# A transformer block on one core: turning the LayerNorm tiles of the feed-forward parts with VectorE blocks and DMAs through DRAM instead of TensorE

## The chip, the core and the metric

The kernel runs on one core of a Trainium2 chip. The core has five engines that run side by side, each with its own instruction stream in program order: TensorE (PE, matrix products; its weight loads are shown as PEld), VectorE (DVE), ScalarE (ACT), GpSimd (POOL) and SyncE (SP, which here issues DMAs). They meet by semaphores. Sixteen DMA engines move data between DRAM, the on-chip memory SBUF and, for the engines alone, the accumulator memory PSUM, which has 8 banks of 128 x 512 fp32. The metric is the device time of one execution in microseconds; the time given is a median of runs.

## The reference

All is fp32. Input x is (8, 256, 512): 8 sequences of 256 tokens, 512 features. Four residual parts follow each other:

```
x = x + attn_a(layernorm(x))    # 32 heads of 16, 8 key/value heads, rotary, causal softmax
x = x + ffn(layernorm(x))       # base linear 512x512 + bias, top-2 of 8 experts, LoRA of rank 16
x = x + attn_b(layernorm(x))    # same shape, other weights
x = x + ffn(layernorm(x))       # the same ffn weights again
```

`layernorm` has no learned factors: (x - mean) / sqrt(var + 1e-5) over the features. `ffn` forms gate logits (8 per token), takes the two largest, softmaxes them, and adds 2 * sum over experts of weight * (x A_e) B_e to x base + b. The factor 2 needs no instruction of its own: the two weights are formed against half of their sum.

## The kernel before, in words

**Units and tiles.** Work is cut into 16 units, each one attention part and the feed-forward part behind it, for one sequence: units 0 to 3 are the first attention of sequences 0 to 3, 4 to 7 the second attention of the same, 8 to 15 the same for sequences 4 to 7. Each unit has two tiles of 128 tokens (t = 0, 1). So there are 64 LayerNorm tiles: 32 ahead of attentions ("a") and 32 ahead of feed-forwards ("f").

**A LayerNorm tile** (`layernorm_t`, L623). VectorE takes mean and variance (L631, L633, L635), GpSimd raises to the power -1/2 (L637), VectorE forms the shift (L638), ScalarE writes the normalized 128 x 512 tile xn (L640). A product needs the features on the partitions, so the tile has to be turned: PE makes four 128 x 128 transposes into a PSUM bank (L647), and ScalarE copies the bank into xnT (for "a") or yT (for "f") (L654). There are 3 xn buffers and 2 yT buffers.

**Attention** (`attention`, L658). PE forms keys (L675), values (L686) and queries (L746); VectorE and GpSimd rotate them (L700 to L768); DMAs copy q and parts of the values (L720, L775). Scores are formed twice: once to find the row maxima (PE L801, ScalarE copy L816, GpSimd mask L832, VectorE maximum L846, turned by PE L855, copied by ScalarE L858 and put into q by two DMAs, L862), and once with the maxima in place (PE L887, ScalarE exponential L902, GpSimd mask L913). PE multiplies by the values (L932); ScalarE copies the result to e (L947). The sums of the softmax go by DMA to a small tile (sums, L952), through a reciprocal (L955), by DMA to DRAM (recd, L959) and by DMA back, broadcast (rec, L963); VectorE scales e (L966, L970). PE makes the `wo` product (L978) and VectorE adds it to x (L985).

**Feed-forward** (`ffn`, L989). After the LayerNorm tile comes the bias (GpSimd L994), the gate and low-rank product `gl` (PE L999, copy L1007), a short chain of gating on VectorE and ScalarE (L1018 to L1044), a transpose `lwT` (PE L1049, copy L1053), the base product (PE L1063), the low-rank product `lora` into the same bank (PE L1069), and the sum into x (DVE L1079). yT is read by `gl` and by base.

**What sets the order.** Nothing is issued directly: `plan.add` records 2,955 operations, each with its engine, a cost, what it reads and writes, and the buffers that it takes from and gives back to pools (x, xn, yT, e, big, the PSUM banks, alone or in pairs, and more). `Plan.schedule` then goes through time with these costs, and on each engine picks the ready operation with the smallest rank of a table (`RANKS`); it also deals out buffers as they come free. The instructions are issued in the order so found, so each engine's order is fixed ahead of the run. On SP the DMAs stand in the same way in one line, up to eight outstanding, and a DMA that waits for its data holds those behind it.

Of the kernel before, what the change touches and what calls it, by code (L numbers as in the profile page):

```python
# [15 lines left out]
P = 128  # L16
# [10 lines left out]
CHANGE = {"full": 0.08, "score": 0.16, "value": 0.13}  # L27
APART = 0.07
WINDOW = 3.4
SPLIT = 16  # L30
FIXED = 1.65
QUEUED = 8
# [3 lines left out]
RANKS = """  # L36
0 65 400 0 585 195 130 455 260 680 716 752 788 390 1870 955 2165 3555 325 3195 1105 1655 2615 2760
715 3645 1030 1795 2830 520 650 1240 1520 2905 1725 2255 2685 1280 1338 1680 1738 0 100 200 300 400
500 615 637 676 761 335 396 406 430 491 521 609 680 413 474 484 508 567 597 736 810 1676 1945 1852
2084 2150 2187 2277 2410 2345 2346 2373 2444 2566 2525 2657 2607 876 1407 1609 1674 1796 2515 1053  # L40
1230 1432 1497 1514 2150 3485 3130 2800 2922 3015 3259 3392 3532 3313 3435 3528 3779 3942 4228 4060
3741 3956 3863 4105 4216 4388 4514 4124 4411 4246 4565 4644 4743 4414 4779 4536 4977 5056 5142 5024
5235 5331 5266 5434 5644 5740 5675 5913 6035 6128 6237 6349 6203 6325 6418 6588 6797 6371 6511 6604
6527 6805 6712 6728 6991 6898 7100 7212 7105 7262 7371 7436 7710 7789 7854 8059 7571 8439 8920 9311
6914 7339 7550 7659 7724 8405 8450 8515 8735 8025 9203 9383 9931 9372 9654 9664 9893 9992 10057
10329 10400 11025 10882 11003 11037 11089 11072 11161 11301 11212 11456 11585 11672 11771 10472
12243 12372 10005 10066 10076 10428 10598 10683 10836 10907 11281 11560 11789 11823 11952 11858
11988 12039 12059 12079 12088 12347 12454 11075 12632 12824 1133 1194 1204 1228 1287 1317 1584 1655
824 885 895 919 978 1008 1630 1705 2038 2307 2214 2425 2723 2760 2642 3325 3260 2669 2811 2882 3271
3180 3312 3221 2897 3090 3353 3292 3525 3652 2446 2623 2872 2937 3005 3132 3870 3940 4927 5049 5142  # L50
5262 5522 5713 5229 5351 5444 5655 5766 6163 5995 5623 5745 5838 6004 6115 6522 6354 7487 7643 7736
7845 7924 8090 7237 7457 7364 7566 7645 7804 6620 6697 6728 6793 8328 8574 8605 8670 7781 7996 7903
8105 8371 10039 10254 10161 10480 10689 10978 11202 11109 11463 11585 11678 10375 10590 10497 11152
11436 11694 11859 11968 12033 12233 12405 12340 12610 12168 12990 13178 13600 11834 12009 12166
12470 12275 12670 12780 12715 13010 12698 13390 13590 13965 13829 13890 13900 14611 14932 14967
15090 15208 15067 15814 15935 15969 16021 16004 16057 16108 16128 16148 16157 16720 16763 15426
17193 17306 14026 14087 14097 14480 14539 14845 14947 15039 14933 16624 16745 16836 16947 16871
16983 17054 17034 17074 17083 17374 17411 16829 17479 17620 1055 1116 1126 1150 1211 1241 2400 2475
2794 2855 2865 2953 3059 3108 3267 3362 3472 4031 3648 4149 4302 4339 4327 4215 4280 4354 4423 4494
4872 4913 4679 4629 4573 4750 5025 4964 5135 5395 3838 4221 4449 4682 4723 4850 5594 5529 8080 8202  # L60
8295 9084 9217 9433 8177 8481 8388 8664 8846 9142 8974 8533 8655 8748 9782 10051 10832 10304 8823
9078 8985 9545 9624 9710 9286 9408 9501 9703 9945 10083 11451 11491 11702 11572 11439 11476 11507
11637 12141 12268 12361 12470 12582 12535 12750 12657 12859 13479 14993 15115 15258 14480 14752
14609 15329 15451 15544 15653 15765 14037 14248 14422 14357 14839 14884 14949 15154 14867 15534
17664 18055 16007 16198 16355 16529 16464 16737 16782 16847 17052 16765 17445 19336 19790 18116
18177 18187 18238 18362 18530 18943 19014 18655 19702 19823 19912 20106 20264 20213 20435 20308
20590 20599 22493 22549 20029 22630 23042 19851 20168 20178 20234 20295 20325 20681 20765 20415
20837 21048 21228 21309 21263 21493 21661 21681 21729 22387 22602 22720 21779 22754 22903 1898 1959
1969 1993 2052 2134 3410 3621 2998 3072 3082 4053 4289 4339 4511 4729 7589 7878 7987 8105 8311 8348
8344 8171 8236 10024 8525 8775 8853 8894 8935 9171 5052 5446 5648 5934 5877 8217 8356 8630 8848 8913  # L70
8957 9418 9617 9552 9749 9871 9964 10162 10295 10611 12829 13044 12951 13188 13368 13539 13661 13081
13330 13237 13883 14148 14434 14266 14185 14434 14341 14663 14742 14945 13940 14155 14062 14330
14532 14618 15790 15827 15858 15923 15802 15842 15988 16053 16330 16550 16457 16659 16771 18122
18244 18337 18446 18782 19895 20126 20219 16732 16854 16967 19798 20013 19920 20122 20286 19086
19297 19406 19471 20185 20230 20295 20500 19699 20880 22143 22660 20490 20949 21114 21223 21288
21701 21746 21811 22016 21544 22782 22944 23440 22721 23025 23035 23072 23164 23194 23334 23405
23304 23477 23832 23896 23948 23944 24068 24119 24371 24391 24400 24650 24693 23589 24759 24918
23501 23588 23598 23668 23931 23968 24138 24256 24056 24554 24675 24709 24761 24744 24797 24868
24848 24888 24897 25211 25248 24863 25320 25449 12433 12494 12504 12694 12811 12843 13035 13137
12885 12946 12956 13068 13195 13423 13544 13615 16432 17281 17386 17504 17570 17759 18211 17570  # L80
17635 18361 18140 18290 18602 18643 18480 18430 14577 14770 15166 15231 15248 17697 14287 15152
15354 15419 15436 17570 17831 17896 19234 19390 19483 19592 19725 19947 20393 20515 20608 20717
20828 20999 21060 22505 22627 22738 22847 22961 23103 23177 20740 20955 20862 21064 21143 21272
21089 21329 21216 21438 21517 22166 23322 23362 23573 23443 23937 24040 24071 24136 24041 24163
24306 24415 24541 24662 24877 24784 24986 25195 25564 25798 25705 25223 25345 25438 25859 25981
26074 26183 26295 25424 25612 25786 25721 25986 26031 26096 26301 26014 26681 26863 27238 26246
26437 26594 26768 26703 27172 27282 27217 27487 26968 27867 28705 29096 27299 27360 27370 27394
27453 27483 27838 28085 27571 29631 29842 29910 29962 29945 29998 30049 30346 30366 30375 30598
30635 29743 30877 30999 29157 29218 29228 29254 29482 29512 30091 30162 29617 30719 30930 30964
31016 31060 31069 31120 31140 31160 31169 31253 31303 30234 31520 31675 31077 31753 17367 17428  # L90
17438 17462 17607 17637 18030 18101 17681 17742 17752 17824 17925 17955 18076 18151 21191 21480
21589 21707 21797 21834 22262 21941 21876 21788 22191 22289 22408 22367 22499 22449 18412 18766
19029 18968 19118 21911 18219 18589 18791 18856 18991 22471 22634 22699 22847 23062 22969 23171
23535 23675 23380 23667 23502 23776 23887 24007 24203 32094 32216 32309 32531 32960 33246 33078
35089 35309 35216 35418 35497 35641 34669 34893 34800 35002 35120 35206 33420 33710 33806 33741
36489 36607 36638 36703 36913 37035 37128 37237 37349 37256 37471 37378 37642 38125 37909 38062
38155 38947 39162 39069 38512 38634 38727 38836 38948 38609 38820 38994 38929 39234 39381 39316
39631 39262 40135 40422 40914 39522 39713 39870 39979 40044 40379 40481 40546 40751 40195 41274
41422 41813 40975 41036 41046 41098 41460 41584 41788 41859 41754 42295 42416 42450 42512 42485
42548 42740 42599 42760 42769 42994 43037 41931 43205 43318 41874 41935 41945 42105 42164 42194  # L100
42391 42462 42367 42898 43019 43053 43105 43088 43141 43212 43192 43232 43241 43293 43330 42534
43402 43531 43410 43609 23362 23423 23433 23483 23562 23595 23949 24055 22964 23345 23355 23431
23575 23760 23995 24105 26671 27398 27305 27555 27621 27658 28318 27686 27621 28655 27867 28345
28423 28464 28555 28505 25666 25956 26235 26174 26407 28006 24200 24377 24579 24644 24661 27698
28205 28140 28608 28730 28823 28932 29121 29261 29071 29286 29193 29395 29506 29849 29681 29534
29656 29749 29858 29969 30285 30117 30965 31087 31180 31289 31368 31454 30137 30352 30259 30461
# [112 lines left out]
class Plan:  # L219

# [30 lines left out]
    def prepare(self):  # L259
# [3 lines left out]
        for n, o in enumerate(ops):  # L263
            for d in o[4]:
                self.succ[d].append(n)
# [886 lines left out]
```

## Time and profile before

| | |
|---|---|
| median of 3 runs | 775.36 us (774.79 to 775.76) |
| profiled execution | 773.26 us, span 771.6 us |
| PE busy | 756.0 us, 98% |
| VectorE, ScalarE, GpSimd busy | 505.9, 486.7, 513.6 us (66, 63, 67%) |
| transposes of the 64 LayerNorm tiles (L647) | 256 matmuls, 38.7 us of summed durations |
| copies out of PSUM to yT (L654) | 32, 18.9 us |
| DMA traffic | 36.06 MB, mean 47 GB/s |

The page gives busy time by engine, a chain of work followed back from the last instruction, and groups of instructions with their idle time before and what ended it. Matmuls are pipelined, so summed durations of a group are more than the time that it holds PE. "SPq" rows are DMAs as SP issues them: their duration is that of the issue, not of the transfer. Idle time of an engine other than the one that bounds the kernel costs nothing in itself.

### The profile page before, as it was taken

Reading aid. Unit: us, or ns where it says so; the run is one execution under the profiler, and the core shown is the slowest. Engines: PE = TensorE matmul, PEld = TensorE weight load, DVE = VectorE, ACT = ScalarE, POOL = GpSimd, SP = SyncE. Lnnn points to the kernel's source line nnn. Section 1 sums busy time; section 2 is a strip of 40 time slices with the busy share of each in tenths; the row PEclk is TensorE's granted clock in tenths of the full one; section 3 lists DMA queues with packets and bytes.
Section 4 is the critical chain, followed back from the end, with each engine's and each line's share of the span. In section 5 each row is a group of like instructions: output and inputs, shape, how many; then the busy total and the mean of one; then the engine's idle time right before and its main releaser. Section 6 shows DMA issues by size and latency. Waiting matters only on the chain.

```text
span 771.6 us, 17960 instructions
## 1 busy us (share of the span) xinstructions
PE 756.0 (98%) x7196; PEld 410.9 (53%) x7196; DVE 505.9 (66%) x1035; ACT 486.7 (63%) x700; POOL 513.6 (67%) x495
## 2 busy tenths in 40 slices
PE   8999999999999999999999999999999989999998
PEld 7874555556456464555555465455555434544354
DVE  6574895856698358666557469465975894666564
ACT  4687757756666654685657566764576775657631
POOL 5898894848667586586738467696468974764530
PEclk9999999999999999999999999999999999999999
DMA  9820101101010020202021210020011100110111
GB/s 298 226 77 6 35 28 38 45 16 33 17 48 5 18 61 2 76 31 62 2 72 48 71 49 3 4 62 16 16 34 51 42 4 18 49 44 32 45 32 54
DMA packets 46755, 36.06 MB, mean 47 GB/s; under 512 B 28496, under 2 KB 31568, under 8 KB 46672
## 3 DMA queue, kind: packets, MB, share of 16 engines
q1 hardware_dynamic: 46128, 34.89, 15.0%
q8 instruction: 56, 0.92, 0.5%
q14 instruction: 27, 0.22, 0.1%
q10 hardware_dynamic: 544, 0.03, 0.0%
HBM read 19.71 MB, written 4.72 MB: 32 GB/s over the span
## 4 chain that ended last, share of the span: by engine, by line
PE 89%; DVE 4%; ACT 3%; issue 2%; POOL 2%; DMA 1%; SPq 0%; POOLq 0%; ACTq 0%; DVEq 0%
PE banks L746 14%; PE banks L1063 13%; PE banks L978 13%; PE banks L887 10%; PE banks L932 9%; PE banks L801 9%; PE banks L675 4%; PE banks L686 4%; PE banks L999 4%; PE banks L1069 4%; PE banks L647 3%; DVE nm L846 2%; POOL big L832 1%; ACT big L902 1%; ACT big L816 1%
## 5 line engine op out<-in xcount | busy, mean ns | idle before, releaser
L832 POOL TENSOR_SCALAR_AFFINE_SELECT big<-big 64x1024 f32<-64x1024 f32 (+1 forms) x160 | 172.4, 1078 | 72.3 <-ACT big L816 66.6
L846 DVE TENSOR_REDUCE nm<-big 128x8 f32<-128x1536 f32 (+3 forms) x112 | 184.7, 1670 | 36.3 <-POOL big L832 36.0
L913 POOL TENSOR_SCALAR_AFFINE_SELECT big<-big 64x1024 f32<-64x1024 f32 (+1 forms) x96 | 145.4, 1514 | 80.1 <-ACT big L902 74.9
L816 ACT COPY big<-banks 128x1024 f32<-128x1024 f32 (+1 forms) x164 | 154.9, 998 | 63.3 <-PE banks L801 60.6
L902 ACT ACTIVATE big<-banks 128x1024 f32<-128x1024 f32 (+1 forms) x166 | 156.6, 993 | 42.0 <-PE banks L887 40.7
L746 PE MATMUL banks<-xnT,wqkv 128*128 128x256 f32 x512 | 120.9, 384 | 1.0 <-ACT xnT L654 0.8
L1063 PE MATMUL banks<-base_sb,yT 128*128 128x512 f32 x256 | 117.4, 601 | 0.9 <-ACT big L902 0.7
L978 PE MATMUL banks<-wo,e 128*128 128x512 f32 x256 | 117.2, 601 | 0.4 <-ACT big L816 0.4
L746 PEld LDWEIGHTS banks<-xnT,wqkv 128*128 128x128 f32 x512 | 93.8, 190 | 29.5 <-issue 13.0
L887 PE MATMUL banks<-q,kz 32*64 32x512 f32 (+1 forms) x1536 | 91.7, 537 | 0.2 <-ACT big L902 0.2
L801 PE MATMUL banks<-kz,q 32*64 32x384 f32 (+3 forms) x2048 | 88.4, 442 | 1.8 <-ACT big L816 1.6
L932 PE MATMUL banks<-big,vp 64*32 64x512 f32 (+1 forms) x1536 | 77.2, 522 | 1.2 <-ACT big L902 1.2
L1063 PEld LDWEIGHTS banks<-base_sb,yT 128*128 128x128 f32 x256 | 46.1, 190 | 59.7 <-issue 48.1
L978 PEld LDWEIGHTS banks<-wo,e 128*128 128x128 f32 x256 | 46.4, 190 | 57.6 <-issue 50.8
L637 POOL TENSOR_TENSOR st<-st,neg_half 128x1 f32<-128x1 f32 x64 | 36.6, 573 | 55.1 <-DVE st L635 35.0
L640 ACT ACTIVATE xn<-x,st 128x512 f32<-128x512 f32 x64 | 52.1, 818 | 19.9 <-DVE st L638 19.6
L801 PEld LDWEIGHTS banks<-kz,q 32*64 32x64 f32 x2048 | 36.9, 130 | 42.1 <-issue 16.7
L932 PEld LDWEIGHTS banks<-big,vp 64*32 64x32 f32 x1536 | 26.8, 106 | 52.8 <-issue 37.0
L994 POOL TENSOR_TENSOR x<-x,bias_sb 128x512 f32<-128x512 f32 x32 | 40.6, 1271 | 18.6 <-ACT xn L640 17.3
L966 DVE COPY_PREDICATED e<-half_i,e 128x512 f32<-128x512 uint32 x32 | 33.1, 1036 | 29.9 <-DMA sums<-e 25.3
L766 POOL TENSOR_TENSOR ro<-ro,rtab 128x512 f32<-128x512 f32 x32 | 41.6, 1301 | 14.1 <-DVE ro L760 12.8
L970 DVE TENSOR_TENSOR e<-e,rec 128x512 f32<-128x512 f32 x32 | 32.7, 1021 | 26.7 <-DMA rec<-recd 26.7
(73 smaller groups left out, 877.6 us busy)
## 6 DMA issues: line engine op xcount, KB each, us to landing
q<-q SPq DMA_DIRECT2D x32, 256.0 KB
rec<-recd SPq DMA_DIRECT2D x32, 256.0 KB
x<-in_x SPq DMA_DIRECT2D x16, 256.0 KB
out<-x SPq DMA_DIRECT2D x16, 256.0 KB
big<-in_wqkv_a SPq DMA_DIRECT2D x2, 512.0 KB
wo<-in_wo_a SPq DMA_DIRECT2D x4, 256.0 KB
big<-in_wq_b SPq DMA_DIRECT2D x2, 512.0 KB
base_sb<-in_base_t SPq DMA_DIRECT2D x4, 256.0 KB
```

The source lines that it names most:

```text
L640: add("ACT", 0.82, (u, z + "ln"), lambda: nc.scalar.activation(at("xn", k), xt(b, t), AF.Identity, bias=st(10, 11), scale=st(9, 10)), [xk, ...
L746: nc.tensor.matmul(at("bank", k)[:, (j % 2) * S : (j % 2 + 1) * S], W[:, c, j * P : (j + 1) * P], xnT()[:, c, :], start=(c == 0), stop=(c ...
L801: nc.tensor.matmul(ps[64 * c : 64 * c + 64, base // 256 * 256 : base // 256 * 256 + 2 * dist] .rearrange("p (s k) -> p s k", s=2)[:, :, ba ...
L816: add("ACT", 1.03, (u, f"s1{gr}"), lambda h=h, kb=kb: [nc.scalar.copy(at("big", kb)[:, 2 * h + lo : 2 * h + hi, :], ps) for lo, hi, ps in ...
L832: nc.gpsimd.affine_select(out=v, in_=v, compare_op=ALU.is_ge, fill=MASKED, base=0, pattern=[[0, 2048 // w], [0, blocks * w // 2048], [-1, ...
L846: nc.vector.tensor_reduce(nmv(t)[:, :, m0 : m0 + k, :, g], v, AX.X, ALU.max, negate=True)
L887: nc.tensor.matmul(ps[64 * s : 64 * s + 64, 256 * col : 256 * (col + ng)], kz2()[lo : lo + 32, s, k * P + 64 * h : k * P + 64 * h + 64], q ...
L902: add("ACT", 1.03, (u, f"s2{gr}"), lambda z=z, kb=kb: [nc.scalar.activation(pv_(kb)[:, 2 * z + lo : 2 * z + hi], ps.rearrange("p z (g n) - ...
L913: nc.gpsimd.affine_select(out=v, in_=v, compare_op=ALU.is_ge, fill=0.0, base=0, pattern=[[0, 16 * nm], [1, 64]], channel_multiplier=-1,)
L932: nc.tensor.matmul(ps[s][32 * i : 32 * i + 32, 256 * g : 256 * (g + ng)].rearrange("p (g n) -> p g n", n=256), vp()[64 * s : 64 * s + 64, ...
L978: nc.tensor.matmul(at("bank", ("wo", km)), e()[:, 1, j * P : (j + 1) * P], WO[:, j, :], start=(j == 0), stop=(j == 3),)
L1063: nc.tensor.matmul(ps, at("yT", k)[:, c, :], base_sb[:, c, :], start=(c == 0), stop=False)
```

## The change

For the tiles that a table `TURNED` marks (0 for each "a" tile, 1 for each "f" tile) the transposes on PE and the copy by ScalarE are left out. In their place VectorE turns xn in place inside its 32 x 32 blocks; four DMAs, one for each 32 partitions, write the blocks to their turned places in a DRAM tile of 512 x 128 (runs of 32 numbers, 128 bytes); and one DMA reads the DRAM tile into yT (runs of 128 numbers, 512 bytes). The yT buffer is taken by the read, the xn buffer given back by the writes. Each marked tile has its own DRAM tile (64 are there). All five DMAs are issued by SP.

The scheduler is gone: the operations are sorted by a table of start times (`TIMES`), and buffers and PSUM banks are dealt out by a second table (`LOANS`). So the order of the instructions differs on every engine, not only around the turned tiles. There are 3,083 operations: 32 fewer on PE and on ScalarE, 32 more on VectorE, 160 more on SP, 484 as before on GpSimd.

```diff
+TURNED = "0011001100110011001100110011001100110011001100110011001100110011"
...
-    def schedule(self, rank, limit):
...
     def run(self):
-        self.prepare()
-        rank = [int(z) / 100 for z in RANKS.split()]
-        best = self.schedule(rank, 1e9)
...
+        loans = iter([int(z) for z in LOANS.split()])
+        self.start = [int(z) / 1000 for z in TIMES.split()]
...
+        self.order = sorted(range(len(self.ops)), key=lambda n: (self.start[n], n))
...
         for n in self.order:
...
+            o[3]()
...
+        "scr": tiles(64, [D, P], "scr", dram),
...
+    def turned(k):
+        return int(TURNED[4 * k[0] + 2 * (k[1] == "f") + k[2]])
...
+        way = turned(k)
+        if way != 0:
+            add("DVE", 0.70, (u, z + "lnT"), lambda: nc.vector.transpose(at("xn", k), at("xn", k)),
+                [], [kn])
+            for i in range(4):
+                add("SP", FIXED + 0.5, (u, z + "lnT"), lambda i=i: nc.sync.dma_start(
+                    at("scr", k).rearrange("(j a) (i b) -> i a j b", a=32, b=32)[i],
+                    at("xn", k)[32 * i : 32 * i + 32, :].rearrange("a (j b) -> a j b", b=32)),
+                    [kn] + ([] if i else list(after)), [(kn, "w", i)] + ([] if i else first),
+                    take=[] if i else [("scr", ("scr", k)), *(take if z == "a" else ())],
+                    give=[("xn", k)], kind=0.45)
+            add("SP", FIXED + 1.2, (u, z + "lnT"), lambda: nc.sync.dma_start(
+                dst(), at("scr", k).rearrange("(c p) n -> p c n", p=P)),
+                [(kn, "w", i) for i in range(4)], [key],
+                take=take if z == "f" else [], give=[("scr", k)], kind=0.9)
+        if way == 1:
+            return
```

## The prediction

> **What bounds the kernel now.** I read the page's busy line and chain first, then the table by stage, then the groups of the parts that change, and last the instructions of the final stretch in order of time.
>
> ```profile
> PE 756.0 (98%) x7196; PEld 410.9 (53%) x7196; DVE 505.9 (66%) x1035; ACT 486.7 (63%) x700; POOL 513.6 (67%) x495
> PE 89%; DVE 4%; ACT 3%; issue 2%; POOL 2%; DMA 1%; SPq 0%; POOLq 0%; ACTq 0%; DVEq 0%
> ```
>
> TensorE (PE) is busy 98% of the span and is 89% of the chain that ended last. The stages, with busy time in the column after the length:
>
> ```profile
> 20.00:100.00 80.00, 78.87 (x865) 50.29 (x865) 51.73 (x77) 59.49 (x82) 70.95 (x72) 1.00 0.32 88
> 100.00:600.00 500.00, 498.15 (x4764) 268.72 (x4762) 330.95 (x682) 321.88 (x466) 339.00 (x318) 1.00 0.12 34
> 600.00:660.00 60.00, 54.82 (x595) 27.53 (x601) 43.09 (x73) 41.00 (x57) 41.70 (x39) 1.00 0.07 24
> 740.00:771.60 31.60, 27.89 (x95) 14.31 (x93) 17.19 (x54) 7.05 (x17) 4.89 (x5) 1.00 0.14 49
> ```
>
> From 100 to 600 us PE idles 1.85 us out of 500, at the full granted clock (1.00). So time taken off PE counts in full there, and every new wait of PE costs in full too. Only 600 to 660 and the end have air (5.2 and 3.7 us).
>
> ```profile
> L647 PE MATMUL banks<-ident,xn 128*128 128x128 f32 x256 | 38.7, 277 | 1.6 <-ACT xn L640 1.6
> L654 ACT COPY yT<-banks 128x512 f32<-128x512 f32 x32 | 18.9, 591 | 21.9 <-PE banks L647 21.8
> L760 DVE STREAM_SHUFFLE ro<-banks 128x512 f32<-128x512 f32 x32 | 23.5, 735 | 0.0
> ```
>
> The first two are what is taken away (half of the first). The third is the nearest row to the VectorE transpose that comes in. Last the end of the run, cut to the last `wo` product, its LayerNorm and what follows; columns are start, duration, engine, line:
>
> ```profile
> 750.93 0.60 PE L647 MATMUL banks<-ident,xn 128*128 128x128 f32 x4
> 751.37 3.60 PE L978 MATMUL banks<-wo,e 128*128 128x512 f32 x8
> ...
> 757.74 0.81 ACT L640 ACTIVATE xn<-x,st 128x512 f32<-128x512 f32 x1 [0.51 <-DVE st L638]
> ...
> 759.27 0.60 PE L647 MATMUL banks<-ident,xn 128*128 128x128 f32 x4
> ...
> 761.54 1.09 PE L999 MATMUL banks<-gl_sb,yT 128*128 128x136 f32 x8
> ...
> 768.00 0.69 DVE L1079 TENSOR_TENSOR x<-banks,x 128x512 f32<-128x512 f32 x1 [0.24 <-PE banks L1069]
> ```
>
> The last `wo` ends at 751.37 + 3.60 = 754.97. Its tile is needed by L999 at 761.54, 6.57 us later, and base products fill PE meanwhile. That distance is what the change stretches.
>
> **Removed from PE and ScalarE.** Four transposes stand 0.44 us ahead of what follows them (750.93 to 751.37), so a tile's block occupies PE 0.44 us, not 4 x 277 ns. All but one of the 32 stand before the last `wo`: 31 x 0.44 = **-13.6 us**, in a stretch where PE has nothing to spare. The 32 copies to yT (18.9 us of ACT) go too; ACT is busy 63%, so I count nothing for them. The attention half's 32 tiles keep both.
>
> **Added to VectorE.** 32 transposes at 0.735 (bounds 0.68, the 128x512 sum of L985, and 1.04, L966) = 23.5 us on an engine that is idle 34%. Hidden by that idle time, except in the chain of each tile.
>
> **The new chain of a tile.** The pieces are these:
>
> ```profile
> 218.70 1.33 SPq L720 DMA_DIRECT2D vp<-kvs  x2
> 743.17 1.15 SPq L959 DMA_DIRECT2D recd<-sums  x2
> 745.59 0.61 SPq L963 DMA_DIRECT2D rec<-recd  x1
> 749.86 0.68 DVE L970 TENSOR_TENSOR e<-e,rec 128x512 f32<-128x512 f32 x1
> ```
>
> Two vp issues of many short runs take 1.33, so 0.67 each. The second recd issue starts at 743.75 and the read that waits for it at 745.59, so a small write is seen 1.84 after its issue. The read of rec is used 4.27 after its issue, an upper bound, since VectorE had other work. Now the chain from the end of `wo`: 3.58 to the end of xn (758.55 - 754.97), 0.1 + 0.74 for the transpose, 3 x 0.67 until the fourth write issues, 2.1 until it is seen (1.84 and a little for 512 runs), 2.7 for the read (between 1.84 and 4.27, nearer the low end because rec's read is a broadcast of 256 KB to all partitions and the others are seen in under 2). Sum 11.2, with 0.2 of handing over **11.4 us**, against 6.57 at the end of before. Bounds 10.5 and 13.0.
>
> How fast short runs move: in the stretch 220.00 to 221.30 the DMA engines are 0.49 busy on the vp copies, whose 1,024 runs of 64 bytes take (with the tails beside that stretch) some 15 ns of an engine each. A tile's 2,048 runs of 128 bytes at that are 1.9 us of 16 engines, or 0.48 per write, below the 0.67 between issues. So issue, not movement, sets the pace.
>
> The Trainium skill (VectorE: DVE Perf Modes, "The three transpose paths") speaks against the change: a plain DMA copy that transposes by strides is put at 19 times the 1309 ns of the crossbar for a 128x128 tile. By that an estimate for one LayerNorm tile of four such squares is 100 us and for 32 tiles over 3 ms, and the kernel would be several times slower. Here VectorE turns inside 32x32 blocks, so the runs stay 128 bytes long; the vp row is for half that length, and I go by the row.
>
> **The end.** After the last `wo`, the built order has gl, base, lwT and lora of one tile, then gl, base, lwT and lora of the other: PE has 0.96 + 3.5 + about 1.5 = 6 us to do and then waits until 11.4. From L999 to the end before has 10.06 (771.6 - 761.54). After it is 0.3 shorter, with one lora less and lora straight behind its own lwT. 11.4 + 9.7 = 21.1 against 16.6: **+4.5 us** (3.6 to 6.1).
>
> **The order elsewhere.** The tables replace the whole order, on all engines. I counted PE's work between each tile's `wo` and its first use of yT in both built orders, each product at the time from its start to the next one's in this trace (3.54 for `wo` and base, 1.05 for a block of scores, 1.02 for gl). The median went from 11.7 to 16.9, which covers 11.4; before needed about 6.5. Short of it, besides the last unit (8.2 and 5.7), are the two tiles of unit 11 with 10.0 and 11.1: **+1.4**, since the first one's wait serves the second too (0 to 3). In two more places ahead of the end lora follows its own lwT with nothing between: PE waits for the copy (766.21 + 0.27, after a transpose that ended at 766.17), 0.45 each, **+0.9**. At the start, half a query weight (512 KB) is issued ahead of the first x tile: one issue (0.47) and a share of its transfer, **+1.2** (0.5 to 2.2).
>
> **The queue.** 160 DMAs join SP's 343, in order. A tile holds SP for 4 x 0.67, then until the fourth write is seen (about 2), then 0.6. Behind 22 of the 32 reads stands, directly, a DMA of an attention chain (8 nmT, 8 sums, 5 recd, 1 rec), for which `wo` or the second score products wait. No row shows what that costs. Below: nothing, if each became ready later than the read was issued. Above: the full hold, 1.84 + 0.61 = 2.45 each, 54 us. That no such cost at all comes through I don't believe: counted in the same way, PE's work between the value products and `wo` is 12.5 at least in before and 11.1, 11.4 and 12.1 at the tightest places now, while the chain from the last value product through sums, recd and rec to `wo` takes about 11 (739.27 to 750.54 in this trace). Against the full hold stands that most reads would be issued with their writes nearly landed. I take one slot of the queue each, 0.65 (the mean issue of the rows above): **+14.3 us**. This is the weakest number here.
>
> **Sum.** -13.6 + 4.5 + 1.4 + 0.9 + 1.2 + 14.3 = **+8.7**. The profiled execution took 773.26 (771.6 span and 1.66 around it), 2.1 under the median of the runs, 775.36. So 782.0 profiled, and 784.1 on the scale of the median.
>
> **Rivals.** (1) Faster: what comes off PE stays off. The long median distance speaks for it, ACT's 18.9 us and a PSUM bank per tile too; the tight places above speak against it. With queue and unit 11 at nothing, the start 0.5 and the end 3.6: -13.6 + 0.5 + 0.9 + 3.6 = -8.6, 766.8. It decides if the queue costs under 4 us over all, where the sum passes -1.55. (2) SP's queue becomes the bound: a late DMA makes later ones late, and a read blocks the queue with its data not there. The other terms make -5.6; with half of the hold for each, 22 x 1.2 = 26.4, the time is 796.2, with all of it 824. For it: SP's waits are in order and PE has nothing spare from 100 to 600; against: the order was laid out anew around these DMAs. (3) No change: the queue's term at 5.6 us cancels the rest. (4) The change doing something else: the built order has 32 fewer blocks of L647 and 32 VectorE transposes, so that is excluded.
>
> **How the numbers follow.** About 0.2% (1.55 us) is what a measurement can tell from no change. Faster 0.06 (rival 1), within 0.2% 0.02, 777 to 779 0.04, the forecast's stretch 779 to 798 0.77, above that 0.11 (rival 2). The range is 779 to 798: the queue's term from 9.2 to 28.2 with the others as taken.
>
> **What would show it.** Right: L647 at 128 matmuls, PE busy 742 to 745, PE idle up from 15.6 to about 37; a wait of L999 on DMA of 4 to 6 us in the last 20 us; a transpose near 0.74 each; waits of the reads on their writes, at SP, near 2 us. Wrong: PE idle below 28 (rival 1), or waits of `e` and of the maxima's rows on DMA that grow by tens of us (rival 2). A transpose above 1.04 or writes seen later than 3 us would make every tile late.

## The result and the profile after

The changed kernel takes 783.33 us (median of 4 runs, 781.87 to 784.89), the kernel before 775.08 on the same chip (773.98 to 775.76). The ratio is 1.0095 with a 95% interval of 1.0073 to 1.0116: slower by 8.3 us. The forecast was 784.1. The sum lands close, but several of its terms do not, so that it lands is in part luck; the experiments take the terms apart. The profiled execution of the changed kernel took 782.9 us, with a span of 781.2.

Two lines of the page, the busy time of each engine and the shares of the chain that ended last:

```profile
PE 755.5 (97%) x7068; PEld 399.5 (51%) x7068; DVE 511.8 (66%) x1067; ACT 468.6 (60%) x679; POOL 508.2 (65%) x495
PE 81%; DVE 7%; DMA 4%; ACT 4%; issue 2%; POOL 1%; SPq 1%; ACTq 0%; DVEq 0%; POOLq 0%
```

PE has 128 matmuls less (7,196 before), and yet its busy time is what it was (756.0). Its share of the chain fell from 89% to 81%; VectorE, DMA and ScalarE took it over. The table by stage (length, then busy time and instructions of PE, PE's weight loads, VectorE, ScalarE, GpSimd; then granted clock, share of the DMA engines, GB/s):

```profile
0.00:20.00 20.00, 15.31 (x82) 14.32 (x83) 10.57 (x41) 9.38 (x15) 8.24 (x22) 0.91 0.96 322
20.00:100.00 80.00, 79.28 (x859) 51.00 (x858) 51.80 (x79) 56.38 (x77) 71.45 (x72) 1.00 0.29 81
100.00:600.00 500.00, 495.36 (x4721) 261.31 (x4720) 338.32 (x705) 311.07 (x455) 338.57 (x321) 1.00 0.23 57
600.00:660.00 60.00, 56.31 (x545) 25.88 (x544) 39.02 (x74) 38.15 (x54) 38.91 (x36) 0.97 0.17 41
740.00:781.20 41.20, 30.14 (x118) 13.31 (x102) 18.49 (x62) 5.29 (x13) 3.63 (x4) 0.95 0.28 78
```

From 100 to 600 us PE idles 4.6 us (1.85 before), and in the last 41 us it idles 11.1. The granted clock, 1.00 in every stage of the trace of before, is 0.91, 0.97 and 0.95 in three of these. The groups of the new work: VectorE's transposes, what is left of PE's, and the products that read the turned tile, with the idle time ahead of each group and its releaser at the end of the line:

```profile
L580 DVE STREAM_TRANSPOSE xn<-xn 128x512 f32<-128x512 f32 x32 | 22.6, 705 | 15.5 <-ACT xn L573 14.5 <-DMA rec<-recd 0.9
L600 PE MATMUL banks<-ident,xn 128*128 128x128 f32 x128 | 20.0, 288 | 3.5 <-ACT xn L573 3.3 <-ACT e L900 0.2
L952 PE MATMUL banks<-gl_sb,yT 128*128 128x136 f32 x256 | 36.5, 287 | 5.4 <-DMA yT<-scr 5.4
```

The waits of PE (total, times, longest) name the read of the DRAM tile first:

```profile
PE banks L952 <- DMA yT<-scr: 5.4, 3, 2.5
...
PE banks L931 <- DVE e L923: 1.5, 3, 0.8
...
PE banks L1022 <- ACT lwT L1006: 1.4, 4, 0.4
```

Three waits, and all are in the last 37 us. The instructions there in order of time, cut to the last `wo` (L931), its tile's way through the DRAM tile (L573 normalizes, L580 turns, L583 writes, L589 reads) and what follows. Columns are start, duration, engine, line, and in brackets the idle time before:

```profile
754.88 3.70 PE L931 MATMUL banks<-wo,e 128*128 128x512 f32 x8 [0.51 <-DVE e L923]
...
760.88 1.17 PE L952 MATMUL banks<-gl_sb,yT 128*128 128x136 f32 x8 [2.29 <-DMA yT<-scr]
...
761.43 0.81 ACT L573 ACTIVATE xn<-x,st 128x512 f32<-128x512 f32 x1 [8.24 <-DVE st L571]
...
762.28 0.71 DVE L580 STREAM_TRANSPOSE xn<-xn 128x512 f32<-128x512 f32 x1 [0.88 <-ACT xn L573]
...
763.01 1.94 SPq L583 DMA_DIRECT2D scr<-xn  x4
...
766.58 0.38 SPq L589 DMA_DIRECT2D yT<-scr  x1
...
769.61 1.29 PE L952 MATMUL banks<-gl_sb,yT 128*128 128x136 f32 x8 [2.54 <-DMA yT<-scr]
770.69 5.24 PE L1016 MATMUL banks<-base_sb,yT 128*128 128x512 f32 x8
```

The last `wo` ends at 758.58, and its tile is used 11.03 us later: 3.66 to the end of xn, 0.75 for the transpose, 3.57 from the first write's issue to the read's issue (with 0.02 ahead of it), 3.03 from the read's issue to its use. From the end of `wo` to the end of the span it is 22.6 us, 16.6 before. One thing in it was not foreseen: the last base product takes 5.24 us and not 3.60. The stages around it (granted clock in the third column from the right) say why:

```profile
765.60:769.60 4.00, 1.12 (x2) 0.30 (x2) 0.69 (x1) 0.27 (x1) 0.00 (x0) 1.00 0.49 145
769.60:772.00 2.40, 2.39 (x10) 1.76 (x11) 0.63 (x5) 0.57 (x2) 0.00 (x0) 0.70 0.01 3
772.00:774.00 2.00, 2.00 (x3) 0.67 (x2) 1.32 (x6) 0.00 (x0) 0.00 (x0) 0.50 0.00 0
774.00:776.00 2.00, 2.00 (x6) 0.71 (x4) 0.00 (x0) 0.00 (x0) 0.00 (x0) 1.00 0.00 0
```

After 4 us in which PE worked 1.12, the clock is halved for some 3.4 us. Narrower stretches of the same view show 1.00 from 769.6 to 770.5, 0.50 from 770.6 to 773.9 and 1.00 from 774.0; the 0.70 is a mean over both. The lost 1.64 us are on the path to the end.

The same view shows the clock at 0.50 in two more stretches of this trace, 9.4 to 12.8 and 613.6 to 616.9 us, and at 1.00 in all of PE's work in the trace of before. Three stretches of 3.4 us at half rate are up to 5 of the 9.6 us between the two spans. The clock matters for the medians too. Its mean over a run was 0.991 to 0.993 in the four runs of the changed kernel, and 0.998 on average in the 31 runs of the kernel before that stand beside the experiments. Among those 31, a run takes 0.48 us more for each 0.001 less of mean clock. An estimate from this is that about 3 of the 8.3 us go with the clock.

**Where the time went over the whole run.** The end of a matmul is modelled in the trace (a base product shown with 3.60 us is followed by the next operation 3.44 us after its start), so a wait of a few tenths of a us does not show as idle time; that is why PE's busy time hardly fell. I therefore compare the starts. For each two PE operations in a row the time from start to start is taken, with the lower quartile over both traces for that kind and that successor as its nominal time; what goes beyond it is called lost here. How finely the operations are sorted into kinds moves the entries by 1 to 2 us. The rest of each span, 6.2 us, lies ahead of the first operation and behind the start of the last.

| us | nominal | lost 0 to 20 | 20 to 100 | 100 to 600 | 600 to 740 | 740 to the end | span |
|---|---|---|---|---|---|---|---|
| before | 736.8 | 1.3 | 4.5 | 11.1 | 11.6 | 0.0 | 771.6 |
| after | 723.8 | 4.7 | 2.8 | 19.7 | 12.9 | 11.1 | 781.2 |
| difference | -13.0 | +3.4 | -1.7 | +8.6 | +1.3 | +11.1 | +9.6 |

The 11.1 lost at the end are, start by start: 6.2 in the three waits of `gl` for its read, 2.1 in four low-rank products that stand right behind their own lwT (0.52 each), 0.8 in a wait of `wo` for e, 1.8 from the clock, and 0.2 in small pieces. The two other stretches at half clock make about 1.5 of the 4.7 lost by 20 us and 1.6 of the 12.9 from 600 to 740, more than the whole difference there. From 100 to 600 us no single wait is long: the second scores lose 2.8 more than before, the base products 2.2, `wo` 1.7, the transposes of the maxima 1.3, and `gl`, which waits for the read, 0.1.

### The profile page after: what moved, and what is told of

It is laid out like the page before. It is cut to its first block, busy times and chain, and to the rows that moved or that the text cites. A ratio compares the mean times of both kernels' runs of the same rounds, so it can differ in the third digit from the quotient of the medians.

```text
span 781.2 us, 18003 instructions
## 1 busy us (share of the span) xinstructions
PE 755.5 (97%) x7068; PEld 399.5 (51%) x7068; DVE 511.8 (66%) x1067; ACT 468.6 (60%) x679; POOL 508.2 (65%) x495
## 4 chain that ended last, share of the span: by engine, by line
PE 81%; DVE 7%; DMA 4%; ACT 4%; issue 2%; POOL 1%; SPq 1%; ACTq 0%; DVEq 0%; POOLq 0%
PE banks L699 14%; PE banks L931 12%; PE banks L1016 12%; PE banks L840 10%; PE banks L754 8%; PE banks L885 8%; PE banks L952 4%; PE banks L1022 3%; PE banks L639 3%; PE banks L628 3%; DVE nm L799 2%; ACT big L855 2%; PE banks L600 2%; DMA rec<-recd 2%; DVE st L564 1%
## 5 line engine op out<-in xcount | busy, mean ns | idle before, releaser
L785 POOL TENSOR_SCALAR_AFFINE_SELECT big<-big 64x1024 f32<-64x1024 f32 (+1 forms) x160 | 169.4, 1059 | 83.2 <-ACT big L769 76.9
L799 DVE TENSOR_REDUCE nm<-big 128x8 f32<-128x512 f32 (+3 forms) x112 | 184.3, 1670 | 46.8 <-POOL big L785 40.2
L866 POOL TENSOR_SCALAR_AFFINE_SELECT big<-big 64x1024 f32<-64x1024 f32 (+1 forms) x96 | 142.8, 1489 | 63.0 <-ACT big L855 52.8
L931 PE MATMUL banks<-wo,e 128*128 128x512 f32 x256 | 117.1, 600 | 2.7 <-DVE e L923 1.5
L840 PE MATMUL banks<-q,kz 32*64 32x512 f32 (+1 forms) x1536 | 93.7, 537 | 2.3 <-ACT big L855 2.2
L754 PE MATMUL banks<-kz,q 32*64 32x128 f32 (+3 forms) x2048 | 92.0, 450 | 2.4 <-ACT nmT L811 1.0
L931 PEld LDWEIGHTS banks<-wo,e 128*128 128x128 f32 x256 | 46.6, 191 | 60.1 <-issue 49.2
L573 ACT ACTIVATE xn<-x,st 128x512 f32<-128x512 f32 x64 | 51.9, 821 | 31.7 <-DVE st L571 24.6
L947 POOL TENSOR_TENSOR x<-x,bias_sb 128x512 f32<-128x512 f32 x32 | 40.8, 1274 | 12.9 <-ACT xn L573 11.8
L564 DVE BATCH_NORM_STATS2 st<-x 128x6 f32<-128x512 f32 x64 | 44.1, 691 | 7.6 <-DMA x<-in_x 6.2
L919 DVE COPY_PREDICATED e<-half_i,e 128x512 f32<-128x512 uint32 x32 | 28.5, 891 | 29.2 <-DMA sums<-e 20.8
```

Source lines behind the costliest of these rows:

```text
L564: add("DVE", 0.69, (u, z + "ln"), lambda: nc.vector.bn_stats(st(0, 6), xt(b, t)), [xk], [ks], take=[("st", ("st", k))])
L754: nc.tensor.matmul(ps[64 * c : 64 * c + 64, base // 256 * 256 : base // 256 * 256 + 2 * dist] .rearrange("p (s k) -> p s k", s=2)[:, :, ba ...
L785: nc.gpsimd.affine_select(out=v, in_=v, compare_op=ALU.is_ge, fill=MASKED, base=0, pattern=[[0, 2048 // w], [0, blocks * w // 2048], [-1, ...
L799: nc.vector.tensor_reduce(nmv(t)[:, :, m0 : m0 + k, :, g], v, AX.X, ALU.max, negate=True)
L840: nc.tensor.matmul(ps[64 * s : 64 * s + 64, 256 * col : 256 * (col + ng)], kz2()[lo : lo + 32, s, k * P + 64 * h : k * P + 64 * h + 64], q ...
L866: nc.gpsimd.affine_select(out=v, in_=v, compare_op=ALU.is_ge, fill=0.0, base=0, pattern=[[0, 16 * nm], [1, 64]], channel_multiplier=-1,)
```

## The experiments

The runs were made in three groups. Each ratio is against runs of the kernel before beside them, whose medians were 775.30 (the first four experiments), 776.25 (the next three) and 776.14 us (the last two). The profiled execution of before, 773.26 us, lies some 2 to 3 us under these, so differences between spans come out smaller than those between medians when a kernel is faster.

**The order without tables made for the change.** The turned tiles stay; only `TIMES` and `LOANS` are others. They hold the order that the scheduler of before finds with its old ranks, the new operations having the rank of the transposes that they replace.

```diff
 TIMES = """
-1240 620 620 0 3100 5580 0 3720 1860 13100 13460 13820 14180 2480 11020 4340 11720 25220 26740 17620
+1 650 4001 2 5850 1950 1300 4550 2600 6800 7160 7520 7880 3900 18700 9550 21650 35550 3250 31950
...
 LOANS = """
-0 0 2 1 3 1 7 5 1 1 7 0 0 0 6 4 0 0 0 5 0 2 1 1 19 2 3 55 19 3 1 19 37 4 55 10 0 10 28 1 0 0 5 1 1
+0 0 2 1 4 1 7 7 0 0 6 0 1 1 5 4 0 0 0 7 0 6 1 55 1 2 0 46 1 3 1 1 28 4 1 28 0 19 37 1 0 0 4 1 1 37
...
```

> The turned tiles as in the changed kernel, but the order found by the old scheduler with its old ranks (each new VectorE and SP operation gets the rank of the transposes that it replaces). Theory A (the new tables are what hides the longer chain: in the changed kernel most tiles have 15 us of PE work between wo and the first use, where the shortest chain measured is 11.0): in an order made for a chain of 6.6 us many distances are too short and SP's line blocks, so much slower than the changed kernel, 800 to 840 us. Rival B (the order matters little, PE's removed work and the end decide): 780 to 790 us.

Measured: 844.78 us, ratio 1.0896 (1.0848 to 1.0944). Theory A, and a little beyond its range. Stage 100 to 600 us and the last 44 us:

```profile
100.00:600.00 500.00, 477.08 (x4310) 244.22 (x4308) 327.25 (x669) 284.62 (x409) 314.05 (x298) 0.98 0.22 54
...
800.00:843.70 43.70, 32.44 (x95) 15.80 (x93) 20.81 (x70) 6.68 (x16) 5.71 (x6) 0.92 0.29 74
```

PE idles 22.9 us in the middle instead of 4.6. By the count above, 52.8 us are lost there instead of 19.7, and 32.9 from 600 to 740. So the tables of the changed kernel, order and buffers together, save some 61 us; without them the change would cost eight times as much as it does (69.5 us against 8.3). In the list of waits PE stands 9.0 us on the reads of turned tiles themselves (5.5 at `gl`, 3.5 at base) and more on other engines; part is the granted clock, whose mean was 0.970 and 0.974 in these two runs. What the order does beside delaying the chains is not separated.

**The last unit back on PE.** Only unit 15's two tiles are turned by PE as before; the other 30 stay.

```diff
-TURNED = "0011001100110011001100110011001100110011001100110011001100110011"
+TURNED = "0011001100110011001100110011001100110011001100110011001100110000"
...
```

> Only the two tiles of the last unit go back to TensorE (transposes and ScalarE copy placed where the read stood); all else keeps the tables' order. Theory A (the end of the run costs 6.0 us of span: L952 waits 2.29 and 2.54 us for the read, and the base product after the second wait runs at a granted clock of 0.5 to 0.7 and takes 5.24 instead of 3.60): these go, two blocks of 0.44 and their copies come back: 4 to 6 us less than the changed kernel, 777.5 to 779.5, and the granted clock in the last 20 us is 1.00. Rival B (what ends the run is the last wo and VectorE's chain, the waits only move): under 1.5 us less, 782 to 783.5.

Measured: 779.88 us (10 runs), ratio 1.0054 (1.0037 to 1.0070). That is 3.5 us off the 783.33 of the 32 tiles, between the theories and nearer A. The end of this run:

```profile
756.62 3.60 PE L931 MATMUL banks<-wo,e 128*128 128x512 f32 x8
...
761.32 1.20 PE L952 MATMUL banks<-gl_sb,yT 128*128 128x136 f32 x8 [0.67 <-ACT yT L607]
...
769.37 3.70 PE L1016 MATMUL banks<-base_sb,yT 128*128 128x512 f32 x8
```

The two long waits for the read and the slow base product are gone, and from the last `wo`'s end to the end of the span it is 18.2 us and not 22.6. The loss in the stretch from 740 us on falls from 11.1 to 5.1. The medians show less than these 6.0, partly because this trace lost 1.0 more at its start and 1.4 more from 100 to 600 us, where its clock was 0.50 from 8.3 to 15.0 and from 431.6 to 434.9. So the end costs 3.5 to 6 us of the 8.3, and about half of the changed kernel's loss sits in two of its 32 tiles.

**Does the clock fall because PE idles?** Transposes of the identity that nobody reads are put ahead of the last unit's two `gl`, 16 and 18 of them.

```diff
+FILL = (16, 18)
...
+            if u == len(units) - 1:
+                def pe_fill(k=k, t=t):
+                    for _ in range(FILL[t]):
+                        nc.tensor.transpose(at("bank", ("fill", k))[:, 0:P], ident, ident)
+
+                add("PE", 0.11 * FILL[t], (u, "fill"), pe_fill, ["ident"], [(u, "fill", t)],
+                    take=[("bank", ("bank", ("fill", k)))], give=[("bank", ("fill", k))])
```

> The changed kernel with idle transposes of the identity into a free bank (16 and 18 of them, about 1.8 and 2.0 us) put on TensorE ahead of the two gl products of the last unit, where PE waits for the read. Nothing waits for their result. Theory A (the clock falls because PE stood idle): the granted clock in the last 12 us stays 1.00, the last base product takes 3.6 instead of 5.24, and the run is 1.5 to 2.0 us shorter, 781.3 to 781.8. Rival B (the base product is slow for another reason, such as the DMAs to the output): it still takes over 5, and the time is that of the changed kernel or up to 0.5 us more.

Measured: 782.83 us (4 runs), ratio 1.0104 (1.0068 to 1.0139); profiled execution 781.34, 1.6 less than that of the changed kernel. In its table by stage the clock stays at full, and the last base product takes 3.60 again:

```profile
768.00:770.00 2.00, 1.16 (x10) 0.92 (x9) 0.00 (x0) 0.00 (x0) 0.00 (x0) 1.00 0.71 234
770.00:772.00 2.00, 2.00 (x11) 1.30 (x10) 0.63 (x5) 0.57 (x2) 0.00 (x0) 1.00 0.00 0
```

This one trace agrees with theory A: with PE at work the clock stayed at 1.00. The `gl` still waits for its read, so only the clock's part comes back. On the medians that is 0.5 us, between the two theories, and the spread of the runs does not tell it from nothing.

**What a hold of SP costs.** Four more writes stand behind each read. They go from the base weights to a DRAM tile that nobody reads, in the form of the changed kernel's own writes.

```diff
+            def read_and_more():
+                nc.sync.dma_start(dst(), at("scr", k).rearrange("(c p) n -> p c n", p=P))
+                for i in range(4):
+                    nc.sync.dma_start(
+                        lent["scr2"][2 * u + t].rearrange("(j a) (i b) -> i a j b", a=32, b=32)[i],
+                        base_sb[32 * i : 32 * i + 32, 0, :].rearrange("a (j b) -> a j b", b=32))
+
+            add("SP", FIXED + 1.2, (u, z + "lnT"), read_and_more,
+                [(kn, "w", i) for i in range(4)] + [("base", 0)], [key],
```

> Behind each of the 32 reads SP issues four more writes of the same form to DRAM that nobody reads (128 more DMAs), so that what stands behind a read is issued some 1.5 to 2 us later; the tile's own chain is not longer. Theory A (the prediction's term: a DMA behind a read costs PE what it is late, 22 such): 22 x 1.5 or more, 30 to 45 us slower than the changed kernel, 813 to 828. Rival B (most such DMAs have slack; the body's 8 us of extra PE waits are of the order and of PSUM banks, not of the queue): 0 to 10 us slower, 783 to 793.

Measured: 793.22 us, ratio 1.0231 (1.0187 to 1.0275), just above theory B. In the trace these 128 DMAs are mostly issued 0.55 us apart (median), each read is followed by 2.5 us more of SP on average, 81 us in all, and the run is 10 us longer: 0.31 us per read, an eighth of the hold. Theory A, the forecast's way of pricing, would make it 22 x 2.5 = 55 us. An estimate by this proportion, which one run can't show to hold for shorter holds, puts the 14.3 us of the forecast at about 3. The queue is not free, but what stands in it behind a read has slack.

**The start.** The first tiles of x go ahead of half of the query weight in SP's queue, as they did before.

```diff
 TIMES = """
-1240 620 620 0 3100 5580 0 3720 1860 13100 13460 13820 14180 2480 11020 4340 11720 25220 26740 17620
+620 0 620 0 3100 5580 1240 3720 1860 13100 13460 13820 14180 2480 11020 4340 11720 25220 26740
...
```

> The changed kernel with the first three loads of SP in another order: the two tiles of the first x ahead of the half query weight. Theory A (the start's delay goes through to the end, since PE has little idle time later): VectorE's first statistics start at 3.7 instead of 5.8, PE's first transposes at 6.8 to 7.5 instead of 9.7, and the run is 1.5 to 2.5 us shorter, about 781. Rival B (what PE does at the start is then limited by the query weight or caught up between 20 and 100 us, where the changed kernel's PE lost 1.7 us less than before's): under 0.7 us of difference, 782.6 to 783.8.

Measured: 784.69 us, ratio 1.0110 (1.0091 to 1.0129): no gain, theory B. The trace of this run shows where it stops:

```profile
3.69 0.69 DVE L564 BATCH_NORM_STATS2 st<-x 128x6 f32<-128x512 f32 x1 [1.68 <-DMA x<-in_x]
...
7.39 0.69 DVE L564 BATCH_NORM_STATS2 st<-x 128x6 f32<-128x512 f32 x1 [1.38 <-DMA x<-in_x]
8.00 0.20 DVE L571 TENSOR_SCALAR st<-st 128x1 f32<-128x1 f32 x1
...
9.10 1.97 PE L600 MATMUL banks<-ident,xn 128*128 128x128 f32 x8 [2.98 <-ACT xn L573]
```

The first statistics start at 3.69 as in the kernel before (3.70; 5.80 in the changed one). But the second tile's shift (L571, 8.00) stands on VectorE behind the statistics of a third tile, whose x lands at 7.39. PE transposes at 9.10; it was 9.73 in the changed kernel and 6.83 before. So 0.6 us came back of 2.9. This trace lost 2.6 us more from 600 to 660 us, where the edit is not, but the clock is:

```profile
600.00:660.00 60.00, 56.16 (x521) 25.78 (x519) 37.32 (x69) 36.96 (x52) 36.97 (x34) 0.91 0.16 37
```

It was 0.50 from 612.9 to 623.0 here, and from 613.6 to 616.9 in the changed kernel. What a start with both tiles early would be worth stays open.

**Nothing turned at all.** The order of before, with the 32 tiles' PE transposes and copies taken out and nothing put in; the products read a constant yT.

```diff
+    for z in lent["yT"]:
+        nc.gpsimd.memset(z, 0.5)
...
-        way = turned(k)
-        if way != 0:
...
-        if way == 1:
+        if turned(k):
             return
```

> The order of the kernel before, with the 32 feed-forward LayerNorm tiles not turned at all: no transposes, no copies, no DMAs; the products read two yT buffers that are filled once with a constant, so the output is not the reference's. It measures the term of the prediction that stands for PE's removed work alone, against the kernel before. Theory A (PE is the bound, each block holds it 0.44 us): 13.6 to 15 us less than before, 760 to 761.7. Rival B (the rest of the order keeps its own pace, and part of what PE gains turns into waits for the copies and masks of the scores): 4 to 10 us less, 765 to 771.

Measured: 766.29 us against 776.25, ratio 0.9869 (0.9841 to 0.9898): 10.0 us less, between the theories and at the edge of B. Stage 100 to 600 us, whose line before showed 498.15 us of PE:

```profile
100.00:600.00 500.00, 494.02 (x4760) 262.52 (x4767) 340.79 (x691) 314.46 (x449) 343.45 (x324) 1.00 0.12 36
```

The order of every engine is that of before with these operations missing. PE's nominal time falls by 14.1 us, but 8.0 more are lost (100 to 600: 17.0 instead of 11.1), and the span gets 6.1 shorter, between a short execution of before and one of this kernel that is 0.9 above its median. PE runs ahead and waits for other engines: the first scores lose 2.2 us more than before, `wo` 1.5, the maxima's transposes 0.8, with no DMA added anywhere. The longer ones show in the list of waits, 2.4 us of the first scores on ScalarE's copies (1.6 before) and 1.9 of the maxima's transposes on VectorE (0.9 before). This is the ceiling of the change as long as the other engines' order is what it was: about 10 us, 0.31 per tile and not 0.44. From 100 to 600 us 5.9 us of loss come here without a turned tile, against 8.6 in the changed kernel; that they are the same loss is not shown, since the orders differ.

**One write instead of four.** The tile goes to DRAM in runs of 2 KB by one DMA. Its blocks then do not reach their turned places; only the time is of use.

```diff
-            for i in range(4):
-                add("SP", FIXED + 0.5, (u, z + "lnT"), lambda i=i: nc.sync.dma_start(
...
+            add("SP", FIXED + 0.5, (u, z + "lnT"), lambda: nc.sync.dma_start(
+                at("scr", k).rearrange("(p a) n -> p (a n)", a=4), at("xn", k)),
+                [kn] + list(after), [(kn, "w", 0)] + first,
```

> The changed kernel's order, with one write of the whole tile (runs of 2 KB, not turned through DRAM, so the output is not the reference's) in place of the four writes of 128-byte runs: 96 fewer DMAs on SP, the same bytes, a chain shorter by about three issues of 0.38 us. Theory A (the queue has slack: the body's 8 us of extra waits are the tables' order): only the end gets shorter, by 1 to 1.5 us for each of the last two reads together with the clock's loss, 780 to 782. Rival B (the queue and the four writes make the body's waits): the waits between 20 and 740 us fall to those of before, 8 us less and the end's gain, 773 to 775.5.

Measured: 781.62 us against 776.25, ratio 1.0078 (1.0049 to 1.0107). By the count, 20 to 740 us lose 36.6 instead of 35.4, nothing less, and the end 7.5 instead of 11.1: theory A. At the end the tile is used 9.23 us after its `wo`, 1.8 less, so the wait is short, and the base product that follows runs at full clock:

```profile
768.84 1.19 PE L943 MATMUL banks<-gl_sb,yT 128*128 128x136 f32 x8 [0.87 <-DMA yT<-scr]
769.88 3.60 PE L1007 MATMUL banks<-base_sb,yT 128*128 128x512 f32 x8
```

So the 96 extra writes and their short runs cost nothing that is seen before the end. The wait of the read for the last write's data stays (1.7 us at the end here, 1.6 in the changed kernel), so its price is not tested by this.

**Only tiles with distance.** The old order and ranks, with seven tiles turned by VectorE and DMAs: "f" tiles for most of which PE already has much work between their `wo` and their `gl`. The order found so puts some twenty other operations elsewhere than before.

```diff
-TURNED = "0011001100110011001100110011001100110011001100110011001100110011"
+TURNED = "0000000100100000001000000000000000110000001100000000000000000000"
...
```

> The order of the old scheduler with its old ranks, and only seven of the 32 feed-forward tiles turned by VectorE and DMAs: the first or second tiles of units 1, 2, 4, 8 and 10, six of which have 16 us or more of PE work between wo and the first use in the order of before, so that a chain of 11 us fits without a new order. Theory A (where the distance is there, a tile taken off PE pays its 0.44 us): 7 x 0.44 = 3.1 less than before, or about 2.2 if a third turns into waits as where all tiles were left out; 772 to 773.5 against 775.3. Rival B (the queue and VectorE cost as much as PE gains even then): 775 to 778.

Measured: 773.85 us (7 runs) against 776.14 (12 runs), ratio 0.9971 (0.9956 to 0.9986). The time is just above theory A's range; the difference is in it. It is faster than both kernels, than that of before by 2.3 us (1.1 to 3.4), or 0.33 for each tile. That is what a tile brought where nothing was turned at all (0.31), so no price of the chain is seen on these seven. In the trace no wait of PE on a read is left and the loss at the end is 0.0; its span (773.8) says nothing of the gain, since the profiled execution, 775.48, is the longest of the seven.

**More tiles, with the order moved for them.** 18 tiles, 7 of them "f" and 11 "a", with the ranks of some operations shifted so that each has its distance.

```diff
-TURNED = "0011001100110011001100110011001100110011001100110011001100110011"
+TURNED = "0000000100101000011000000000110010110000101110001100110000000000"
...
```

> Eighteen tiles of both kinds (11 ahead of attentions, 7 ahead of feed-forwards) turned by VectorE and DMAs, in an order with ranks shifted for them; the other 46 stay on TensorE, among them both of the last unit. Theory A: 18 x 0.44 = 7.9 off PE, of which two thirds stay, about 5 less than before: 770 to 771.5. Rival B (every new chain is a new place for a wait, as in the changed kernel): 774 to 777.

Measured: 773.52 us (5 runs), ratio 0.9965 (0.9952 to 0.9979), between the theories. It too beats both, that of before by 2.6 us, but it can't be told from the seven. The busy line of its page, and its row of transposes:

```profile
PE 753.9 (98%) x7124; PEld 402.5 (52%) x7124; DVE 522.4 (68%) x1053; ACT 476.7 (62%) x682; POOL 515.1 (67%) x495
L576 DVE STREAM_TRANSPOSE xn<-xn 128x512 f32<-128x512 f32 x18 | 12.5, 701 | 3.4 <-ACT xn L569 3.3
```

In the traces nominal time fell by 7.0 us and lost time grew by 7.2. The eleven tiles added to the seven bring their time off PE, but no more than a few tenths of it can be seen in the medians.

## Why the prediction was right, and where not

- **Direction and size: right.** 784.1 forecast, 783.33 measured; the chain of a tile, the end and the time off PE were the right things to look at.
- **The sum: in part luck.** Put -10.0 for PE's work, 3 for the queue, 6.0 for the end, 1.0 for the low-rank products and 1.7 for the start, as found below, and nothing for unit 11, and it makes about +1.7, where +8.3 was measured. Some 6 to 7 us lie in none of the forecast's terms as they measure. The clock may be a part of them; they are not separated.
- **Off PE, -13.6: the time was about right, its worth was not.** The nominal time fell by 13.0. But "time taken off PE counts in full there" is the step that failed: with the blocks merely taken out, 10.0 us come (14.1 nominal in the traces). The 1.85 us of idle time in the stage were no evidence that the others keep up: from start to start PE lost 11.1 us there even before, in waits too short to show as idle time.
- **The queue, +14.3: the mechanism is there, the term was several times too large.** A hold of 2.5 us behind every read costs 10 us, so one slot of the queue costs about 3 for all tiles by the estimate above, and three writes less per tile bring nothing before the end. It was called the weakest number, and it was. From 20 to 740 us the changed kernel lost 8.2 us more than before for whatever reason, and one without a turned tile, in the old order, almost as much; the term had 14.3 for the queue alone.
- **The end, +4.5 (3.6 to 6.1): measured +6.0.** The chain was forecast at 11.4 and took 11.03. Writes were cheaper (1.94 us for four issues, 0.49 each and not 0.67) and the read dearer (3.03, not 2.7). The 9.7 from `gl` to the end became 11.6, and 1.64 of that is the clock, which was not in the sum. The end is the largest single place of the trace, where the forecast had the queue; putting the last two tiles back on PE gives back 3.5 us of the medians.
- **Unit 11, +1.4: not seen.** Its first `gl` starts 2.93 us after its read was issued and 0.87 after its nominal turn on PE. But this lies in the stretch at half clock: the two blocks of scores ahead of it took 1.81 and 1.92 us, 1.04 each at full clock. The waits list no read there.
- **The low-rank product right behind its lwT, +0.9: right,** 0.52 each at 743.01 and 753.25.
- **The start, +1.2 (0.5 to 2.2): +3.4 until 20 us, of which 1.7 came back by 100 us.** x came 2.1 us later, not about 1, and PE's transposes 2.9 later; about 1.5 of the 3.4 is the half clock from 9.4 to 12.8.
- **The transposes of VectorE, 0.735: 0.705.** That they cost nothing outside the chains is not shown.
- **PE busy 742 to 745 and 37 us idle: wrong.** 755.5 and 25.7. The forecast's own sign for rival 1 was idle time below 28, and it would have misled: lost time between starts grew by 22.6 us while the idle time grew by 10.1. Two other signs came: `gl` waits 4.8 us for its reads in the last 21 us, and the fourth write of the last tile is seen 2.1 us after its issue.
- **Rivals.** Faster (766.8) did not come. With nothing put in place of the transposes 766.29 was measured; that the two numbers agree is chance, since the rival had 13.6 us off PE and 3.6 for the end. The 17 us between that run and 783.33 are chain, order and clock. Comparing these two traces, of the 15.7 us between the spans 11.1 are lost at the end, 2.5 in the first 20 us, 3.0 from 100 to 740; from 20 to 100 us 2.0 less is lost, and the nominal time is 1.1 longer. SP's queue as the bound (796 to 824) did not come; even with four more DMAs per tile the time is 793.
- **The page that spoke against the change.** From the factor 19 and the 1309 ns of the Trainium skill (VectorE: DVE Perf Modes, "The three transpose paths") the prediction estimated 100 us per tile for a copy that transposes by strides. The page gives the time for bf16, and the factor for a large stride of the innermost dimension of the destination. The measured chain is 11.03 us, and the writes and the read in it 6.6. With the blocks turned on VectorE ahead of the copy, the factor does not show. The same page's rule to use TensorE for a 128x128 transpose ("Rules for kernel authors") agrees with the last unit, where going back to PE gave 3.5 us.

Left open: which part of the remaining 3.0 us from 100 to 740 is the other order, the buffers, or the queue. By kinds it is the second scores (+2.2 against the run with nothing turned, 100 to 600 us) and the base products (+2.0); that it is the order of bank use is only argued. The changed kernel's order with PE's transposes left in was not tried, nor that order with nothing turned, so what the order alone is worth beside the turned tiles is open.

## What to carry to other kernels

A longer chain in place of work on the bounding engine paid here for tiles whose result is wanted late, and cost time for the last ones of the run; so count the bounding engine's work between producer and consumer tile by tile, and change those with room. The order decided more than the operation: the same 32 turned tiles cost 8 us with an order made for them and 69 without. And an engine that is busy 99% of a stage is not proof that time taken off it comes back in full; the engines close behind it keep a part, here some 4 of 14 us. And compare the granted clock of two kernels before the rest of a small difference is explained.

## What the runs showed of the hardware that was not expected

PE's granted clock fell to 0.50 for some 3.4 us behind 4 us in which PE had worked 1.12, and the product that came next took 5.24 us instead of 3.60; with idle transposes, 16 and 18 ahead of the two `gl`, it stayed at 1.00. The halving from 613.6 us came with no gap of PE over 1.15 us in the 9 us ahead of it, while the kernel before had a gap of 2.24 up to 633.8 us and kept 1.00. The length of the gap alone does not decide: with the four more writes per read the product behind a wait of 2.15 us was slow, and in the run with x first the one behind a wait of 2.28 was not, while the one behind 2.35 was:

```profile
773.00 1.17 PE L960 MATMUL banks<-gl_sb,yT 128*128 128x136 f32 x8 [2.15 <-DMA yT<-scr]
774.00 5.29 PE L1024 MATMUL banks<-base_sb,yT 128*128 128x512 f32 x8
```

```profile
763.40 1.17 PE L952 MATMUL banks<-gl_sb,yT 128*128 128x136 f32 x8 [2.28 <-DMA yT<-scr]
764.41 3.60 PE L1016 MATMUL banks<-base_sb,yT 128*128 128x512 f32 x8
...
771.95 1.19 PE L952 MATMUL banks<-gl_sb,yT 128*128 128x136 f32 x8 [2.35 <-DMA yT<-scr]
772.98 5.29 PE L1016 MATMUL banks<-base_sb,yT 128*128 128x512 f32 x8
```

The Trainium skill (TensorE: Matmul & The Clock Gate, "Part 1: The HAM clock gate (the "warmup" mystery)") puts the fall to half behind an idle window of about 3.4 us, in windows that run freely against the program. The half rate, its length of 3.4 us and a time that varies from run to run agree with these rows; but gaps shorter than its window were enough here, and the measurement decides.
